# Reordering a neighbour-limited graph layer on one Trainium2 core: one landing rule for all loads, two count banks, the last tile in three loads

## The chip, the cores and the metric

The kernel runs on one core of a Trainium2 chip. A core has five engines that run side by side, each its own list of instructions in order: TensorE (PE, with PEld for its weight loads), VectorE (DVE), ScalarE (ACT), GpSimd (POOL) and SyncE (SP), which here only issues DMAs. Sixteen DMA engines move data between HBM and the on-chip memory SBUF; matrix products land in PSUM[...]. The metric is the device time in microseconds (us), lower is better; a time is the median of several runs.

## The reference

The layer normalises each of 4096 rows of 64 numbers, multiplies by a 64 x 64 matrix, and then sums over neighbours. Only the last 100 neighbours of a row count, and the one that lies k places before the last has the weight 2 to the power of minus k:

```python
    support = input @ weight
    mask = (adj != 0).astype(support.dtype)
    rank = jnp.cumsum(mask, axis=1)
    deg = rank[:, -1:]
    k = jnp.minimum(deg, float(MAX_NEIGH))
    pos = rank - (deg - k)
    w = mask * jnp.where(pos > 0, DECAY ** (k - pos), 0.0)
    out = w @ support + bias
...
    h = jnp.maximum(_layernorm(x, axis=-1), 0.0)
    x = x + _L0_gnn_ref(h, adj, L0_gnn_weight, L0_gnn_bias)
```

`adj` is a 4096 x 4096 matrix of float32, 67.1 MB, and nearly all that the kernel reads.

## The kernel before

**Tiles.** `adj` is taken in 32 tiles of 128 rows (2 MB each). A tile's 4096 columns are handled as eight blocks of 512. Two tiles make a pair u (16 pairs), four tiles a group g (8 groups) that shares one PSUM bank `acc`.

**Stages of a tile.** Each is a small function; the line of its instruction in the profile is given.

1. `load` (L295, SP): a DMA of the tile into one of four buffers `a_sb`. Tiles 0, 1, 28, 29, 30 and 31 are loaded in two halves, the others whole: 38 loads. A load into a buffer waits until the tile four earlier has been converted.
2. `convert` (L496, DVE): float32 to one byte per element, 64 or 65, into `m`.
3. `flip` (L506, DVE): transposes 32 x 32 blocks of packed words into the mask `mt`.
4. `totals` (L512, PE): counts the neighbours in each strip of the tile.
5. `split` (L517, ACT): takes the two bytes of each count apart, into `sums`.
6. `suffix` (L526, PE): sums the counts from each strip to the end of the row.
7. `clamp` (L530, DVE): limits them, into `behind`.
8. `place` (L538, L542, PE): adds to each element's strip count its place within the strip, into four PSUM banks `v`.
9. `weigh` (L551, ACT): four exponentials per tile turn `v` into weights `wk`; tile 31's are done in three parts (12 instructions), cut by `PARTED`.
10. `aggregate` (L559, PE): 32 products per pair, in eight tasks of four, add `wk` times the supports `hr` into `acc`.

**End of a group.** `drain` (L572, ACT) adds the bias, `turn_back` (L580, PE) transposes, `finish` (L586, DVE) adds the input, `store` (L590, SP) writes rows out. The last group is drained in two halves; there are nine drains, all on ACT, and four stores.

**Head.** Before the first weights the kernel builds constants (`constants`, and `order_of` on POOL, L375 to L389, which makes `near`, `rest` and `far` for `suffix`), normalises `x` (`turn`, `center`, `square`, `relu`, `spread`, `root`, `power`) and makes the supports (`support`, `scale`, `first`, `second`). The first weights' buffer also holds the normalisation's data, so that tile 2's weights wait for all four `second`.

**Order.** The order on each engine is made at build time by `plan()`: it holds a list of tasks with engine, duration (`hold`), time to result (`lag`), needs and buffers (`tasks()`), plays them in time, and at each step takes, among the tasks that could start within a small window (`WAIT`), the one with the lowest due time from the table `DUE`. For a load it reckons when its data is there from the data's size. PSUM is shared between `v` (`NV` = 6 banks), counts, suffixes and turned results `t` (`NB` = 1 bank) and `acc` (one bank). `warm` puts filler products on PE where the plan leaves it idle.

Of the kernel before, what the change touches and what calls it, by code (L numbers as in the profile page):

```python
# [8 lines left out]
F32 = mybir.dt.float32  # L9
F32R = mybir.dt.float32r  # L10
BF16 = mybir.dt.bfloat16
F16 = mybir.dt.float16
# [19 lines left out]
STEP = {t: 4 for t in (0, 1, 28, 29, 30, 31)}  # L32
LOADS = [(t, h, h + STEP.get(t, 8)) for t in TILES for h in range(0, 8, STEP.get(t, 8))]

PARTLY = {31}
PARTED = (0, 1, 0, 2), (1, 2, 0, 1), (1, 2, 1, 2)
DRAINS = [(g, 0, 4, True) for g in range(7)] + [(7, 0, 2, True), (7, 2, 4, True)]
STORES = [(0, 0, 16), (1, 0, 12), (1, 12, 14), (1, 14, 16)]
NA, NM, NT, NW, NV, NB = 4, 4, 4, 2, 6, 1

DUE = {
    "fetch": [-1003, -1847],
    "load": [65, 1148, 1192, 1344, 890, 882, 1059, 807, 177, 1469, 585, 426, -306, 496, -49, 266, 921, 615, 495, 273,
    509, 817, 887, 432, 1250, 832, 1156, 645, 31, 863, 872, 512, 638, 869, 1362, 792, 926, 1009],
    "load_rest": [-481],
    "turn": [-213, 892, -361, 828, -409, -147, 168, -107],
    "turned": [-404, -273, 1152, 128, 503, 511, 433, -263],
    "center": [-857, -641, -1350, -827],
    "square": [139, -1681, -2148, -2029],
    "relu": [217, 890, -64, 143],  # L50
    "spread": [-1274, -1134, -743, -201],
    "support": [458, 166, -823, -732],
    "scale": [31, 1087, -17, 582],
    "root": [-38],
    "power": [-305],
    "constants": [-1199, 288],
    "order_of": [1110],
    "count": [174],
    "counted": [-242],
    "first": [1030, 859, 446, 134],  # L60
    "second": [869, 310, 488, 149],
    "convert": [799, 235, 213, 621, 871, 221, 1137, 339, 665, 170, 840, 839, 269, 846, 1322, 763, 1208, 992, 1053, 1092,
    755, 1566, 506, 1283, 1017, 914, 1881, 1297, 1713, 1456, 1930, 1878, 1817, 1254, 2527, 1603, 1404, 1849],
    "flip": [755, -234, 295, -127, 442, -299, 314, 236, -95, 42, 943, 437, 1189, 848, 1722, 445, 670, 663, 1043, 1071,
    1018, 1159, 1502, 907, 1558, 1730, 1512, 1723, 625, 1907, 1701, 1739, 1719, 1519, 1418, 1515, 1365, 795],
    "totals": [163, 587, 208, 187, -888, 339, 133, -152, 475, 1157, 159, 135, 674, 545, 1071, 817, 439, 1024, 1281,
    1461, 443, 2052, 963, 1181, 926, 1932, 1537, 584, 1513, 1671, 1316, 1615],
    "split": [-294, -174, -1849, -575, -454, -698, -618, -971, -742, -275, 300, 6, -214, 155, -90, -143, 509, 616, 114,
    395, 584, 524, 615, 13, 506, 320, 818, 391, 1992, 1302, 1105, 460],
    "suffix": [265, 470, 626, 553, 76, 351, -120, 701, -560, 193, 222, 311, 159, 444, 810, -221, 772, 1294, 1743, 886,  # L70
    718, 429, 591, 1159, 1296, 2185, 1511, 1501, 2001, 1496, 2127, 1546],
    "clamp": [-739, 475, 354, 317, -585, 294, 102, -276, 538, 118, 920, -398, 130, 1157, 352, 866, 900, 81, -363, 492,
    698, 1569, 702, 757, 515, 1132, 736, 1149, 1495, 1590, 1729, 1541],
    "place": [841, 96, 498, 879, 824, 837, 808, 522, 1103, 1914, 1312, 1548, 862, 1225, 743, 1302, 1785, 1644, 1994,
    1697, 1566, 1560, 1577, 1633, 2537, 1922, 1847, 2364, 2393, 2364, 1714, 1845],
    "weigh": [1655, 1181, 868, 631, 1236, 404, 1584, 1443, 897, 269, 877, 841, 328, 1501, 418, 1096, 1670, 1095, 1290,
    1045, 1295, 1247, 1314, 999, 672, 1559, 1035, 1631, 1070, 1779, 1431, 1276, 2029, 1311, 1734, 1852, 1556, 1640,
    1599, 1881, 1168, 1820, 1423, 545, 1375, 1271, 1659, 2299, 2395, 2281, 2155, 2139, 2062, 2491, 1666, 1651, 1902,
    1875, 1618, 2485, 1751, 1754, 2523, 1796, 2184, 2358, 1409, 2593, 2132, 1541, 1713, 2047, 1583, 1456, 1562, 2282,
    1641, 1846, 1727, 2021, 2924, 2344, 2590, 1925, 1978, 2498, 1946, 1761, 2622, 1817, 2190, 1884, 1953, 2032, 2057,  # L80
    2381, 2020, 2701, 1854, 2394, 2313, 2255, 1976, 2259, 1957, 2012, 1591, 2429, 2382, 2260, 2365, 3172, 2928, 2044,
    3150, 1958, 2643, 2675, 2150, 3338, 2587, 2729, 2343, 2953, 1990, 2517, 2778, 3358, 2745, 2645, 3479, 2076, 3183,
    2758, 2299, 2866],
    "aggregate": [254, 1326, 1623, 59, 522, 1349, 93, 1245, 247, 484, 1268, 1686, 2132, 1190, 2358, 448, 974, 1308,
    1356, 611, 856, 1518, 486, 1545, 1236, 918, 398, 1827, 1513, 1406, 1117, 1500, 1296, 1193, 452, 1811, 1260, 1164,
    1961, 1568, 1038, 1010, 1127, 1422, 1532, 1050, 1941, 1756, 685, 1493, 1977, 1124, 1719, 1240, 1199, 787, 2328,
    1076, 2631, 1964, 1500, 1168, 989, 1906, 1959, 931, 1528, 1194, 1746, 1676, 1766, 1637, 1602, 1588, 2104, 1990,
    1832, 1942, 1495, 1697, 1592, 2020, 1907, 2085, 1379, 1230, 1622, 2213, 2061, 2515, 2853, 1453, 2287, 1736, 1377,
    1679, 1972, 1745, 1669, 2617, 3235, 2571, 1770, 2567, 1656, 2752, 2666, 1678, 2311, 2453, 2712, 2395, 2976, 2826,
    2628, 2119, 2143, 2488, 2511, 1602, 2160, 1962, 2594, 2032, 2291, 2585, 1920, 2821],  # L90
    "drain": [82, 374, 29, 620, 400, 1392, 1843, 1544, 1599],
    "turn_back": [572, 1129, 645, 1544, 2558, 1512, 1987, 1280, 2435],
    "finish": [79, 927, -547, 514, 1225, 592, 1061, 2342, 2532],
    "store": [8458, 8834, 7981, 9977],
}
WAIT = 250, 60, 150, 60, 0
PE, DVE, ACT, POOL, SP = range(5)


def tasks():  # L100
# [12 lines left out]
    for n, (t, _, _) in enumerate(LOADS):  # L113
        task("load", (n,), SP, n, 0, 0, [("convert", m) for m in range(n) if LOADS[m][0] == t - NA])
    task("load_rest", (), SP, 4, 0, 0, [("load", 2)])
    for h in range(2):
        for t0 in range(0, 16, 4):
            task("turn", (h, t0), PE, 0, 430, 680, [("fetch", h)], ("v", ("turned", h, t0)))
            task("turned", (h, t0), ACT, 0, 480, 640, [("turn", h, t0)])
    for n in range(4):  # L120
        task("center", (n,), PE, 1, 860, 1060, [("turned", 1, 12)], ("v", ("relu", n)))
        task("square", (n,), ACT, 1, 480, 640, [("center", n)])
        task("relu", (n,), ACT, 2, 480, 640, [("square", n)])
    for n in range(4):
        task("spread", (n,), PE, 2, 850, 1050, [("square", n)])
    for n in range(4):
        task("support", (n,), PE, 15, 890, 1090, [("relu", n), ("power",)], ("v", ("scale", n)))
        task("scale", (n,), DVE, 10, 610, 730, [("support", n), ("power",)])
# [7 lines left out]
    for i in (0, 2, 1, 3):  # L136
        task("first", (i,), ACT, 15, 520, 650, [("scale", i % 2 * 2 + 1), ("support", 3)])
        task("second", (i,), DVE, 15, 610, 740, [("first", i)])
# [496 lines left out]
```

## Time and profile before

| what | value |
|---|---|
| time, median of 3 runs | 188.82 us (188.42 to 188.97) |
| the profiled execution's own time | 188.37 us |
| its span in the profile | 186.7 us |
| PE busy | 164.9 us (88% of the span) |
| DVE busy | 146.8 us (79%) |
| ACT busy | 152.1 us (82%) |
| POOL busy | 18.9 us (10%) |
| HBM read | 68.19 MB |
| `weigh`, 124 full ones | 1081 ns each, 118.8 us in all |
| `convert`, 26 whole tiles / 12 halves | 2637 ns / 1375 ns each |
| `flip`, 26 whole tiles / 12 halves | 1241 ns / 706 ns each |

A profile is one execution; the 188.37 us contain its span of 186.7 us and what lies around it. Busy time is the time in which an engine has at least one instruction at work. Neighbouring instructions of one engine overlap a little in the records, so the distance from one start to the next (here called a slot) is shorter than a duration: four `weigh` in a row, 1081 ns each, start some 905 ns apart. The page cuts the span into 40 slices, one digit each, in tenths of busy share; the chain of work that ended last goes back from the last instruction to what released each one.

### The profile page before, as it was taken

What the parts mean: (1) busy time and instruction counts of PE and PEld (TensorE: products, weight loads), DVE (VectorE), ACT (ScalarE), POOL (GpSimd) and SP (SyncE); (2) the same over time, 40 slices, a digit from 0 to 9 for tenths busy, and PEclk for the clock granted to TensorE, in tenths of its full rate; (3) what the DMA queues carried; (4) which work ended last, traced back from release to release, by engine and by line L of the source; (5) the groups of instructions that cost most, each with busy time, mean ns of one, the idle gap of its engine ahead of it and who ended that gap; (6) DMA issues with size and microseconds to landing.
All of it is one profiled execution on the core that took longest, in us unless ns stands there. A gap on an engine that the chain in (4) does not pass through costs nothing.

```text
span 186.7 us, 4747 instructions
## 1 busy us (share of the span) xinstructions
PE 164.9 (88%) x2080; PEld 127.3 (68%) x2080; DVE 146.8 (79%) x152; ACT 152.1 (82%) x198; POOL 18.9 (10%) x57
## 2 busy tenths in 40 slices
PE   7999699647989899889998997999898979897982
PEld 5957367435857768667676775877775858685881
DVE  3187499999999997799797899879798989993100
ACT  2773176912999999699999999999969799999951
POOL 7899500000000000000000000000000000000000
PEclk9997569999999999999999999999999999999999
DMA  6999999999999999999999999999999999940020
GB/s 202 390 427 435 435 420 425 416 428 428 428 414 428 434 414 432 428 414 442 411 428 428 418 432 421 418 446 411 428 421 414 413 420 416 417 201 0 12 90 16
DMA packets 6597, 69.55 MB, mean 373 GB/s; under 512 B 944, under 2 KB 1200, under 8 KB 1712
## 3 DMA queue, kind: packets, MB, share of 16 engines
q1 hardware_dynamic: 6416, 69.21, 88.4%
q8 instruction: 16, 0.26, 0.6%
q10 hardware_dynamic: 160, 0.03, 0.1%
q14 instruction: 5, 0.04, 0.1%
HBM read 68.19 MB, written 1.05 MB: 371 GB/s over the span
## 4 chain that ended last, share of the span: by engine, by line
ACT 36%; PE 32%; DVE 15%; POOL 10%; issue 5%; POOLq 0%; ACTq 0%
ACT wk L551 29%; PE acc L559 19%; DVE m L496 7%; ACT sums L517 5%; PE ps L526 5%; PE po L580 3%; DVE mt L506 3%; PE v L542 2%; DVE behind L530 2%; PE v L538 2%; PE tot L512 2%; ACT acc_sb L572 1%; DVE wk L472 1%; DVE hr L482 1%; POOL where L414 1%
## 5 line engine op out<-in xcount | busy, mean ns | idle before, releaser
L551 ACT ACTIVATE wk<-v 128x1024 fp32r<-128x1024 uint8 (+2 forms) x136 | 123.2, 1028 | 2.3 <-PE v L542 2.1
L496 DVE TENSOR_SCALAR m<-a_sb 128x4096 uint8<-128x4096 f32 (+1 forms) x38 | 84.8, 2238 | 5.0 <-DMA a_sb<-in_adj_dram 5.0
L559 PE MATMUL acc<-wk,hr 128*128 128x256 f32 x512 | 74.6, 291 | 3.7 <-ACT wk L551 2.2
L559 PEld LDWEIGHTS acc<-wk,hr 128*128 128x128 f32 x512 | 64.0, 188 | 10.6 <-ACT wk L551 4.3
L506 DVE STREAM_TRANSPOSE mt<-m 128x1024 f32<-128x1024 f32 (+1 forms) x38 | 40.7, 1072 | 0.4
L517 ACT ACTIVATE sums<-tot 128x512 f16<-128x512 uint8 x32 | 20.3, 634 | 16.4 <-PE tot L512 16.4
L530 DVE TENSOR_SCALAR behind<-ps,excess 128x256 f16<-128x256 f32 x32 | 15.4, 481 | 14.1 <-PE ps L526 13.9
L526 PEld LDWEIGHTS <-far 128*128 128x128 f16 x224 | 17.9, 101 | 1.9 <-POOL far L389 1.0
L526 PE MATMUL ps<-sums,far 128*128 128x224 f16 (+6 forms) x224 | 18.5, 225 | 0.7 <-POOL far L389 0.7
L512 PE MATMUL tot<-mt,band 128*32 128x256 f16 x256 | 13.5, 288 | 5.3 <-DVE mt L506 4.3
L538 PE MATMUL v<-behind,where 32*128 32x256 f16 x256 | 13.6, 276 | 2.7 <-DVE behind L530 2.3
L542 PE MATMUL v<-mt,tri 32*32 32x512 f16 x512 | 14.5, 401 | 0.0
L586 DVE TENSOR_TENSOR xr<-po,xr 128x256 f32<-128x256 f32 (+1 forms) x9 | 3.5, 393 | 12.4 <-PE po L580 12.3
L423 PE MATMUL none<-junk 128*128 128x256 bf16 x74 | 11.9, 318 | 1.1 <-DVE junk L307 1.1
L512 PEld LDWEIGHTS <-band 128*32 128x32 f16 x256 | 4.1, 95 | 11.3 <-DVE mt L506 6.1
L423 PEld LDWEIGHTS <-junk 128*128 128x128 bf16 x87 | 8.8, 109 | 3.8 <-DVE junk L307 1.1
L526 PE MATMUL ps<-sums,near 128*128 128x256 f16 x32 | 9.2, 286 | 2.0 <-ACT sums L517 1.8
L572 ACT ACTIVATE acc_sb<-acc,bias_sb 128x512 f32<-128x512 f32 (+1 forms) x9 | 6.1, 679 | 5.4 <-PE acc L559 5.4
L580 PE MATMUL po<-both,acc_sb 128*128 128x64 f32 x64 | 8.7, 275 | 1.9 <-DVE behind L530 1.3
L580 PEld LDWEIGHTS po<-both,acc_sb 128*128 128x128 f32 x64 | 7.8, 191 | 2.8 <-DVE behind L530 1.5
L538 PEld LDWEIGHTS <-where 32*128 32x128 f16 x256 | 4.5, 92 | 7.5 <-issue 4.7
L542 PEld LDWEIGHTS <-tri 32*32 32x32 f16 x512 | 4.4, 88 | 6.9 <-issue 6.9
(86 smaller groups left out, 91.0 us busy)
## 6 DMA issues: line engine op xcount, KB each, us to landing
a_sb<-in_adj_dram SPq DMA_DIRECT2D x26, 2048.0 KB, 15.3
a_sb<-in_adj_dram SPq DMA_DIRECT2D x12, 1024.0 KB, 13.2
xr<-in_x_dram SPq DMA_DIRECT2D x2, 512.0 KB, 3.9
out_dram<-xr SPq DMA_DIRECT2D x1, 512.0 KB, 17.1
out_dram<-xr SPq DMA_DIRECT2D x1, 384.0 KB, 2.3
out_dram<-xr SPq DMA_DIRECT2D x2, 64.0 KB, 1.6
w<-in_L_gnn_weight_dram ACTq DMA_DIRECT2D x2, 16.0 KB, 5.8
bias_sb<-in_L_gnn_bias_dram SPq DMA_DIRECT2D x1, 0.2 KB, 18.8
```

Source lines behind the costliest of these rows:

```text
L423: nc.tensor.matmul(idle[0][:, idle[1]:idle[1] + 2 * P], junk[:, :P], junk, start=not accs, stop=not accs, skip_group_check=True)
L496: nc.vector.tensor_scalar(words[n][:, :(k1 - k0) * P, :].rearrange("p (h q) e -> p h e q", q=P), tiles[t][:, k0 * W:k1 * W].rearrange("p ( ...
L506: nc.vector.transpose(to[:, k0:k1], m_v.rearrange("p (h c l) -> p h c l", c=4, l=SUB))
L512: nc.tensor.matmul(tot[SUB * c:SUB * (c + 1), :V], band[:, SUB - 12 - 4 * a:2 * SUB - 12 - 4 * a], masks[t][:, c, :, a], start=(a == 0), s ...
L517: nc.scalar.activation(sums8[t], pts.pop((t, "n"))[:, :V].bitcast(U8).rearrange("p (i f) -> p f i", f=4)[:, :2, :], AF.Copy, bias=-136.0)
L526: nc.tensor.matmul(o, l, m, start=(k == 0), stop=(k == len(todo) - 1), skip_group_check=True)
L530: nc.vector.tensor_scalar(behind[t], pts.pop((t, "s"))[:, :V], excess, float(MAX_NEIGH), op0=ALU.subtract, op1=ALU.min)
L538: nc.tensor.matmul(vs[t, j][:, a, :], where[q, a, :], behind[t][q, :], start=(a == 0), stop=False, skip_group_check=True)
L542: nc.tensor.matmul(vs[t, j][SUB * c:SUB * (c + 1), :, :], tri[q, q], masks[t][q, c, :, :].rearrange("p i a -> p a i"), start=False, stop=T ...
L551: nc.scalar.activation(wts[u][:, s0:s1, 8 * a0:8 * a1, i, j, :], v[:, s0:s1, 8 * a0:8 * a1], AF.Exp, scale=-LN2, bias=-38.0 * LN2)
L559: nc.tensor.matmul(accs[g][:, at:at + 2 * P], hr[:, h * 4 + 2 * a + s, :, :].rearrange("p s d -> p (s d)"), wts[u][:, s, 8 * a + h].rearra ...
L580: nc.tensor.matmul(pts["o", d][:, k, :], sums[d][:, k * P:(k + 1) * P], both, start=True, stop=True)
```

## The change

The order of all engines is made anew, with another table `DUE` and with other durations and needs in `tasks()`. Its parts:

- A load's data counts as there some time after the nominal end of its transfer, by a rule `late` that is the same for every tile and grows over the run (850, 1750, 3200 ns).
- Tiles 28, 29 and 30 are loaded whole; tile 31 is loaded in three pieces (blocks 0 to 3, 4 and 5, 6 and 7), each flipped by itself. There are 36 loads.
- Each whole tile is converted in two instructions of four blocks, and flipped in one.
- `t` has two banks (`NB` = 2), of which a tile uses half (`half()`), and `v` has five (`NV` = 5). `behind` has four buffers.
- `weigh`'s parts of tile 31 go by blocks (0 to 3, 4 and 5, 6 and 7), and `aggregate`'s eight tasks of a pair go by block.
- `order_of` runs on DVE; `constants` for `where` works on 8 columns in place of 256 and spreads them in its last instruction; the bias is loaded by two DMAs; `both` and `less` are made in a task `stack`.
- The drains stay as they were: all nine on ACT. `encode` and `take` are new functions for doing weights on DVE, and `HALF_UNITS` for half tiles; both sets are empty, so that neither is used.

The diff's core:

```diff
-STEP = {t: 4 for t in (0, 1, 28, 29, 30, 31)}
-LOADS = [(t, h, h + STEP.get(t, 8)) for t in TILES for h in range(0, 8, STEP.get(t, 8))]
-
-PARTLY = {31}
-PARTED = (0, 1, 0, 2), (1, 2, 0, 1), (1, 2, 1, 2)
+CUTS = {0: ((0, 4), (4, 8)), 1: ((0, 4), (4, 8)), 31: ((0, 4), (4, 6), (6, 8))}
+HALF_UNITS = set()
+
+LOADS = [(t, h0, h1) for t in TILES for h0, h1 in CUTS.get(t, ((0, 8),))]
+PIECES = LOADS
+UNITS = [(t, 0, 8) for t in TILES]
+
+PARTS = {31: ((0, 4), (4, 6), (6, 8))}
+QUICK = set()
...
-NA, NM, NT, NW, NV, NB = 4, 4, 4, 2, 6, 1
+NA, NM, NT, NW, NV, NB = 4, 4, 4, 2, 5, 2
...
-    task("order_of", (), POOL, 1, 3500, 3600, [("constants", 0)])
+    task("order_of", (), DVE, 1, 2950, 3050, [("constants", 0)])
+    task("stack", (), DVE, 2, 600, 700, [("order_of",)])
...
+def late(at):
+
+    return 850 if at < 17000 else 1750 if at < 104000 else 3200
...
             lag = max(landed - at, 2450) + dma_ns(f, args)
             landed = at + lag
+            lag += late(landed)
...
-    bhpool = ctx.enter_context(tc.tile_pool(name="bhpool", bufs=2))
+    bhpool = ctx.enter_context(tc.tile_pool(name="bhpool", bufs=4))
...
-        nc.sync.dma_start(bias_sb[:D], bias.rearrange("(d o) -> d o", o=1))
+        b = bias.rearrange("(d o) -> d o", o=1)
+        for d0, d1 in ((0, 8), (8, D)):
+            nc.sync.dma_start(bias_sb[d0:d1], b[d0:d1])
...
     def order_of():
-        vec = nc.gpsimd
+        vec = nc.vector
...
+    def half():
+        return ps_t.tile([P, V], F32, tag="t", name="sums")
...
-    def convert(n):
-        t, k0, k1 = LOADS[n]
-        words[n] = bpool.tile([P, N // E, E], U8, name="m8")
+    def convert(n, i):
+        t, h0, h1 = PIECES[n]
+        if i == 0:
+            words[n] = bpool.tile([P, N // E, E], U8, name="m8")
+        k0, k1 = 4 * i, min(4 * i + 4, h1 - h0)
...
-    def aggregate(u, k):
+    def aggregate(u, h):
...
-        a, s = k // 4, k // 2 % 2
-        for h in range(k % 2 * 4, k % 2 * 4 + 4):
-            nc.tensor.matmul(accs[g][:, at:at + 2 * P], hr[:, h * 4 + 2 * a + s, :, :].rearrange("p s d -> p (s d)"),
-                             wts[u][:, s, 8 * a + h].rearrange("p i j r -> p (i j r)"), start=(k == h == 0),
-                             stop=(k == h == 7), skip_group_check=True)
+        order = order_in(u)
+        for e in range(4):
+            a, s = e // 2, e % 2
+            nc.tensor.matmul(accs[g][:, at:at + 2 * P], hr[:, h * 4 + e, :, :].rearrange("p s d -> p (s d)"),
+                             wts[u][:, s, 2 * h + a].rearrange("p i j r -> p (i j r)"), start=(h == order[0] and e == 0),
+                             stop=(h == order[-1] and e == 3), skip_group_check=True)
```

With the new order the instructions near the end stand as follows (a number is the tile, for `aggregate` the pair and the block):

```
VectorE  convert 30 (two), clamp 29, flip 30, convert 31 (three), clamp 30, flip 31 (three), clamp 31, finish (three)
ScalarE  weigh 29 (first), split 30, weigh 29 (two), drain 6, weigh 29 (last), weigh 30 (first), split 31, weigh 30 (three), weigh 31 (four of the first part), drain 7, weigh 31 (eight), drain 8
TensorE  aggregate 13.3 to 13.5, place 29, aggregate 13.6, totals 30, aggregate 13.7, suffix 30, place 30, totals 31, aggregate 14.0 to 14.2, suffix 31, turn_back 6, aggregate 14.3, place 31, aggregate 14.4 to 14.7, 15.0, 15.1, turn_back 7, aggregate 15.2 to 15.7, turn_back 8
```

Before, tile 30 is converted and flipped in two halves with tile 29's clamp behind the second convert, the drain of group 6 stands one `weigh` earlier, and TensorE turns group 6 back after it has placed tile 31.

## The prediction

> **What bounds the kernel now.** I read four views in this order: the row of DMA slices, the times at which single loads land, the waits of ScalarE, and last the chain that ended last.
>
> The DMA row of the page and stretches of 1 us near its end (columns: length, then busy time of PE, PEld, DVE, ACT and POOL with counts, the granted clock, the DMA share, GB/s):
>
> ```profile
> DMA  6999999999999999999999999999999999940020
> ...
> 162.00:163.00 1.00, 1.00 (x10) 1.00 (x10) 0.96 (x2) 1.00 (x3) 0.00 (x0) 1.00 0.96 397
> 164.00:165.00 1.00, 1.00 (x12) 0.93 (x8) 1.00 (x3) 1.00 (x3) 0.00 (x0) 1.00 0.74 303
> 166.00:167.00 1.00, 1.00 (x15) 0.90 (x8) 0.97 (x2) 1.00 (x2) 0.00 (x0) 1.00 0.36 147
> ```
>
> The DMA engines are full from about 4 us to 163 us and then thin out, one after another, over some 3 us. No reordering of compute can end this stream earlier; only what comes after it can shrink.
>
> The line of the loads, asked for the two halves of tile 30 and then of tile 31: issue times, and issue to landing.
>
> ```profile
> L295 SPq DMA_DIRECT2D a_sb<-in_adj_dram x2: 327/376/426, 145.6 to 146.0; - x2
> DMA to landing us min/median/max: 13.3/14.3/15.4
> ...
> L295 SPq DMA_DIRECT2D a_sb<-in_adj_dram x2: 328/377/426, 149.7 to 150.1; - x2
> DMA to landing us min/median/max: 14.1/15.2/16.3
> ```
>
> Tile 30 is complete at 146.0 + 15.4 = 161.4 us and tile 31 at 150.1 + 16.3 = 166.4 us; 186.7 - 166.4 = 20.3 us of the span come after the last mark.
>
> ScalarE in order of time, three of its lines:
>
> ```profile
> 45.46 0.60 ACT L517 ACTIVATE sums<-tot 128x512 f16<-128x512 uint8 x1 [3.44 <-PE tot L512]
> 46.09 7.44 ACT L551 ACTIVATE wk<-v 128x1024 fp32r<-128x1024 uint8 x8
> ...
> 138.96 1.03 ACT L551 ACTIVATE wk<-v 128x1024 fp32r<-128x1024 uint8 x1 [1.52 <-PE v L542]
> ```
>
> Tile 2's weights begin at 46.1 us, when the last of the four "second" operations is done. From then ScalarE works off a backlog nearly without a pause, until at 138.96 us it waits 1.5 us for PE: there it has caught up with the data. So the slow start is already paid back 48 us before the end.
>
> The chain that ended last, from 170.8 us (start, length, what):
>
> ```profile
> 168.92 1.84 ACT wk L551 x2
> 170.80 1.69 PE acc L559 x12
> 172.49 0.62 PE ps L526 x9
> 173.11 1.04 PE acc L559 x8
> 174.15 0.33 PE v L538 x8
> 174.47 0.38 PE v L542 x14
> 174.85 1.04 PE po L580 x8
> 175.89 1.49 PE acc L559 x12
> 177.46 0.48 ACT acc_sb L572
> 177.99 0.74 PE acc L559 x4
> 178.72 0.39 PE po L580 x4
> 179.11 3.38 PE acc L559 x28
> 182.58 0.48 ACT acc_sb L572
> ```
>
> From tile 29's last weights the end is one piece of PE work: 64 products of pairs 14 and 15, tile 31's suffix and placing, two turns back and one drain between them, 182.48 - 170.80 = 11.7 us without a gap worth naming, and then a fixed 4.2 us (drain, turn back, finish, store). What the change does to the end is what it does to this start, 170.80 us.
>
> [...] the share falls over 3 us, 0.96 to 0.36, before tile 31 may be read. [...] the trace shows what one bank costs, waits of PE of 0.6 to 0.8 us for a clamp (1.3 us for the turns back, 1.0 us for totals). [...] this is the rival below on five placing buffers, and the trace of before, with six, has 4.4 us of ScalarE idling over 30 tiles.
>
> **The change, part by part.** *Head.* The 13 operations of order_of took POOL from 13.6 to 21.6 us and held up the first suffix (21.68 us); on VectorE, at about 0.2 us each, they are 2.9 us, inside the 3.93 us that it waits there for the first load. POOL's 128x256 operations (1.2, 2.0, 0.7, 2.1 us) shrink to eight columns. By the new order tile 2's weights can begin near 38 us: VectorE reaches the third tile's converts at 23.3, then per the listed order two more tiles and the four "second" operations, each with its old duration. That is 8 us earlier, and worth nothing at the end, since before had caught up at 138.96. Without that cover (if it had not caught up) it would be worth up to the whole 8 us.
>
> *Converts.* 26 whole-tile converts of 2.64 us become pairs of 1.33 us (the pair at 152.48 takes 2.66): +0.5 us over the run, hidden in VectorE's spare time: per tile 2.55 (pair) + 0.40 (clamp) + 1.15 (flip) + 0.1 (finish) = 4.2 us of slots against 4.9 us between marks. Tiles 28 to 30 go back to one load and one flip (1.15 for 2 x 0.64). *Loads.* A tile in halves came every 5.0 us (161.4 to 166.4); whole ones are spaced some 4.9 (67.1 MB over the full stretch), so tile 30's mark comes about 0.2 us earlier, estimate, 161.2; the last mark is then 166.3 with one more small transfer. VectorE read the last half only at 167.35, a microsecond after its mark, so the third piece by itself gains nothing. *The split bias load, drains.* One more tiny transfer among 40 on SP; it lands far ahead of the first drain. All drains are on ScalarE in both: nothing. *Weights.* Same shapes (1024, and 512, 256, 256 elements for tile 31), same 512 products.
>
> *The order at the end*, step by step, with slots from the trace (start to next start). Tile 30 marked 161.2; its two converts 2.55: 163.75; clamp of 29 there (164.29 before); placing starts 0.54 after a clamp does: 164.3; weights start 0.79 after a placing does: 165.1 (165.9 before). ScalarE: weights 0.905, split 0.47, two weights 1.81, drain of group 6 0.57, so tile 29's last weights start at 165.1 + 3.75 = 168.85; its products may start 1.1 us after that (169.70 to 170.80 before): 169.95. VectorE meanwhile: clamp 0.40 and flip 1.15 of tile 30 to 165.3, three converts of tile 31 2.55 to 167.85, clamp of 30 to 168.25, three flips 1.3 to 169.55; totals of 31, which stand before the products on PE, 0.1 + 0.34: 170.0. Both roads meet at 170.0, against 170.80: **0.8 us earlier**. Behind it PE has the same 11.7 us in slightly changed order (turn back of group 6 before tile 31's placing), split of 31 ready at 171.1 for a suffix due at 171.5, placing due at 173.6 with its clamp at 172.4. Sum: span 186.7 - 0.8 = 185.9; the profiled execution would be 188.37 - 0.8 = 187.6; that run lies 0.45 below the median, 188.82 - 0.8 = **188.0 us**.
>
> *New wait.* With five placing buffers instead of six, tile t's placing waits for the third of tile t-1's four weights, not the second; on PE, products and totals queue behind it, and ScalarE waits for those. In my chain the third weights of 29 end at 168.3, just when tile 30's clamp (167.85 + 0.54) allows its placing, and ScalarE wants the result at 169.75: cover 169.75 - 0.79 - 168.4 = 0.55 us. Bounds: 0, or one weights slot, 0.9 us, per tile. I take 0. The second count bank gives back at most the 3.8 us of such waits summed over the run (1.0 + 1.3 + 1.5), none of them in the last chain: 0.
>
> **The rivals.** *A, forecast, 188.0*: the start of the last PE piece moves 0.8 us. *B, nothing: 188.8.* The two roads to 170.0 have no slack between them; small pieces cost a fixed part that the trace of before does not show (it has no 1024-column convert or flip). Four such operations at 0.2 us more each cancel the 0.8. For it: 2 x 0.71 against 1.24 for flips shows a fixed part of 0.18. Against it: slots, not durations, count on a busy engine, and there two halves take 1.28 for 1.15. *C, slower: 190.6.* Five placing buffers. PE must place (0.8 us) while ScalarE has only one weights (0.9) and perhaps a split left; if PE stands in a group of products (up to 1.5 us) at that moment, ScalarE idles s each tile. It has 4.9 - 4.3 = 0.6 us per tile to give and starts 38 us with some 5.6 us to recover over 28 tiles (0.2 each): above s = 0.4 it never catches up and each further 0.1 costs 2.8 us. At s = 0.5 that is 2.8 - 0.8 = 2 us, 190.6 to 190.8. Against it: before idled only 0.15 per tile. *D, better: 187.0*: the 3 us over which the DMA engines finish shrink by 1[...]; tile 30's mark and all behind it come 1 us earlier still. The mirror of it, 1 us later, is 189.0 and lies in the range.
>
> **How the numbers follow.** A 0.50, B 0.23, C 0.19, D 0.08. 0.3% is 0.57 us, what this kernel's measurement can tell: 188.25 and 189.4 are the borders. A falls below 188.25 with two chances in three (0.33) and else within; D is faster (0.08); B is within but for a few chances each way; C is slower, with 0.04 of B. Faster 0.43, same 0.34, slower 0.23. Range: 187.0 (D) to 190.0, which leaves the worse half of C outside. For A and D alone it is 187.0 to 188.5.
>
> **What would show it.** Right: last mark within 0.3 us of 166.3; ScalarE's weights of tile 2 near 38 us; VectorE waiting for loads in the middle of the run; the last unbroken PE stretch starting near 170.0 and ending near 181.7. B: it starts after 170.5 with flips ending after 170. C: PE "v <- ACT wk" waits of tenths of a microsecond in every tile. Wrong altogether: a last mark moved by over 0.5 us, or the 11.7 us changed.

## The result

| | before | after |
|---|---|---|
| time, median (20 runs each) | 188.75 us (188.17 to 189.10) | 190.17 us (188.39 to 191.93) |
| profiled execution, its span | 188.37, 186.7 us | 190.7, 188.7 us |
| first product of pair 14 | 170.80 us | 171.25 us (predicted 170.0) |
| the PE piece from there to its last product | 11.7 us | 13.2 us (predicted 11.7) |

After against before: 1.0076 [1.0059, 1.0093], slower; 188.0 was predicted. (A time is the median of all executions, a ratio rests as a rule on the mean of those within 1.5% of a kernel's fastest, so the two need not agree.) The 2.0 us between the two spans are 0.45 at the start of the piece and 1.5 inside it. Against the span that was forecast, 185.9 us, the 2.8 us are 1.25 at the start and 1.5 inside. The profiled execution of after is one of its slower ones.

The loads did what was predicted. VectorE after (start, length, what, idle time before it and its releaser):

```profile
161.15 2.72 DVE L542 TENSOR_SCALAR m<-a_sb 128x2048 uint8<-128x2048 f32 x2 [0.35 <-DMA a_sb<-in_adj_dram]
163.99 0.48 DVE L587 TENSOR_SCALAR behind<-sums,excess 128x256 f16<-128x256 f32 x1
```

Tile 30 is read on its mark at 161.15 us (predicted 161.2), and tile 29 is clamped at 163.99 (163.75). The last load lands near 166.0 us (166.3). So the DMA side is right to 0.3 us, and what fails comes after it. TensorE after, from there on, and then the chain that ended last:

```profile
161.10 0.74 PE L635 MATMUL acc<-wk,hr 128*128 128x256 f32 x4 [0.17 <-ACT wk L615]
161.78 0.41 PE L560 MATMUL sums<-mt,band 128*32 128x256 f16 x8
162.12 1.21 PE L635 MATMUL acc<-wk,hr 128*128 128x256 f32 x8
...
163.80 1.66 PE L635 MATMUL acc<-wk,hr 128*128 128x256 f32 x12
165.39 0.40 PE L597 MATMUL v<-behind,where 32*128 32x256 f16 x8
```

```profile
169.71 0.57 ACT acc_sb L648
170.28 0.92 ACT wk L615
171.21 0.04 issue
171.25 2.46 PE acc L635 x12
173.71 1.20 PE sums L581 x9
174.91 1.16 PE sums L656 x8
```

In the first, 24 products of pair 13 start at 161.10, when ScalarE has made tile 27's last weights. Tile 29's placing stands behind them and starts at 165.39, 1.4 us after its clamp began. In before 8 products stood between tile 29's clamp and its placing, which started 0.77 us after it:

```profile
163.94 1.18 PE L559 MATMUL acc<-wk,hr 128*128 128x256 f32 x8
164.29 0.48 DVE L530 TENSOR_SCALAR behind<-ps,excess 128x256 f16<-128x256 f32 x1
165.06 0.40 PE L538 MATMUL v<-behind,where 32*128 32x256 f16 x8
```

In the second view of after, 12 products take 2.46 us (1.69 before) and a suffix 1.20 (0.62 before). The granted clock shows a reason, which a later run bears out (after the comma the busy times of PE, PEld, DVE, ACT and POOL with counts, then the clock, the DMA share and GB/s):

```profile
170.00:171.00 1.00, 0.92 (x29) 0.26 (x24) 0.50 (x2) 1.00 (x2) 0.00 (x0) 1.00 0.00 0
171.00:172.00 1.00, 0.75 (x5) 0.75 (x6) 0.00 (x0) 1.00 (x3) 0.00 (x0) 0.92 0.00 0
172.00:173.00 1.00, 1.00 (x7) 1.00 (x6) 0.00 (x0) 1.00 (x3) 0.00 (x0) 0.50 0.00 0
...
175.00:176.00 1.00, 1.00 (x9) 1.00 (x10) 0.43 (x1) 0.36 (x1) 0.00 (x0) 0.87 0.00 0
```

For 3.4 us, 171.85 to 175.26, the granted clock of TensorE is 0.50; in the 3.4 us before it is 1.00. The clock's records show two more such stretches of 3.4 us, at 28.5 and 55.8 us. In the profile of before the clock is 0.50 for 10.2 us on end, 16.2 to 26.4, in the head, and 1.00 from there to 186 us.

The rivals C and B of the prediction are judged by these waits of after (who waits, for whom, us in total, times, longest):

```profile
ACT wk L615 <- PE v L601: 14.9, 13, 3.8
...
DVE m L542 <- DMA a_sb<-in_adj_dram: 7.5, 11, 2.3
...
PE v L597 <- ACT wk L615: 1.8, 6, 0.6
```

VectorE waits for loads in the middle of the run, as forecast, and ScalarE idles more (2.1 us in 2 before). TensorE's placing waits for a buffer only 1.8 us in 6 waits, not in every tile. But three of the six lie at 151, 160 and 170 us, and the first of these, for tile 26, is a step of the chain that ended last:

```profile
151.07 0.37 PE L597 MATMUL v<-behind,where 32*128 32x256 f16 x5 [0.50 <-ACT wk L615]
```

Tile 27's count and placing queue behind it, so the five buffers can have cost up to 0.5 us of the late start; that they did is not shown. B's sign is there as well, a start after 170.5 with flips that end at 170.5. Small pieces account for little of it: tile 30's two converts took 2.72 us, where 2.55 was reckoned. Then tile 30's clamp waited for a suffix on TensorE:

```profile
168.74 0.48 DVE L587 TENSOR_SCALAR behind<-sums,excess 128x256 f16<-128x256 f32 x1 [0.53 <-PE sums L581]
```

### The profile page after: what moved, and what is told of

The parts are those of the page before. It is cut to its first block, busy times and chain, and to the rows that moved or that the text cites. A ratio compares the mean times of both kernels' runs of the same rounds, so it can differ in the third digit from the quotient of the medians.

```text
span 188.7 us, 4792 instructions
## 1 busy us (share of the span) xinstructions
PE 168.1 (89%) x2090; PEld 129.8 (69%) x2090; DVE 150.2 (80%) x190; ACT 153.9 (82%) x198; POOL 6.8 (4%) x43
## 4 chain that ended last, share of the span: by engine, by line
PE 42%; ACT 23%; DMA 17%; DVE 13%; issue 2%; SPq 1%; DVEq 0%; ACTq 0%
PE acc L635 23%; ACT wk L615 18%; DMA a_sb<-in_adj_dram 17%; DVE m L542 8%; PE sums L581 6%; PE v L601 4%; PE sums L656 4%; PE v L597 3%; ACT sums L568 3%; PE sums L560 2%; DVE mt L552 2%; DVE behind L587 1%; ACT acc_sb L648 1%; DVE wk L513 1%; SPq L334 1%
## 5 line engine op out<-in xcount | busy, mean ns | idle before, releaser
L542 DVE TENSOR_SCALAR m<-a_sb 128x2048 uint8<-128x2048 f32 (+1 forms) x65 | 85.7, 1375 | 7.8 <-DMA a_sb<-in_adj_dram 7.5
L635 PEld LDWEIGHTS acc<-wk,hr 128*128 128x128 f32 x512 | 64.8, 190 | 11.7 <-issue 7.3
L552 DVE STREAM_TRANSPOSE mt<-m 128x1024 f32<-128x1024 f32 (+2 forms) x36 | 40.0, 1118 | 0.3
L568 ACT ACTIVATE sums<-sums 128x512 f16<-128x512 uint8 x32 | 20.1, 630 | 6.6 <-PE sums L560 6.3
L587 DVE TENSOR_SCALAR behind<-sums,excess 128x256 f16<-128x256 f32 x32 | 15.1, 477 | 11.3 <-PE sums L581 11.2
L581 PE MATMUL sums<-sums,far 128*128 128x224 f16 (+6 forms) x224 | 18.5, 225 | 0.0
L560 PE MATMUL sums<-mt,band 128*32 128x256 f16 x256 | 13.1, 284 | 1.4 <-DVE mt L552 1.3
L581 PE MATMUL sums<-sums,near 128*128 128x256 f16 x32 | 9.2, 286 | 1.7 <-ACT sums L568 1.2
L656 PE MATMUL sums<-both,acc_sb 128*128 128x64 f32 x56 | 8.4, 296 | 2.2 <-ACT sums L568 2.2
L656 PEld LDWEIGHTS sums<-both,acc_sb 128*128 128x128 f32 x56 | 7.4, 206 | 3.1 <-ACT sums L568 2.4
L581 PE MATMUL sums<-sums,rest 128*128 128x256 f16 x32 | 9.0, 281 | 0.0
```

The costliest lines, as they stand in the source:

```text
L542: nc.vector.tensor_scalar(words[n][:, k0 * P:k1 * P, :].rearrange("p (h q) e -> p h e q", q=P), tiles[t][:, (h0 + k0) * W:(h0 + k1) * W].r ...
L552: nc.vector.transpose(to[:, h0:h1], m_v.rearrange("p (h c l) -> p h c l", c=4, l=SUB))
L560: nc.tensor.matmul(tot[SUB * c:SUB * (c + 1), r], band[:, SUB - 12 - 4 * a:2 * SUB - 12 - 4 * a], masks[t][:, c, r, a], start=(a == 0), st ...
L568: nc.scalar.activation(sums8[t][:, :, r], pts.pop((n, "n")).bitcast(U8).rearrange("p (i f) -> p f i", f=4)[:, :2, r], AF.Copy, bias=-136.0)
L581: nc.tensor.matmul(o, l, m, start=(k == 0), stop=(k == len(todo) - 1), skip_group_check=True)
L587: nc.vector.tensor_scalar(behind[n][:, r], pts.pop((n, "s"))[:, r], excess, float(MAX_NEIGH), op0=ALU.subtract, op1=ALU.min)
```

## The experiments

Times are medians, ratios against before in the same session.

### Clock or order at the end

The letters of the theories in this part are not those of the prediction's rivals. T1 held that the half clock in the tail is the loss, T2 the place of the placings in TensorE's order, T3 the missing sixth placing buffer. First, zero products as filler before tile 30's placing and before pair 14:

```diff
+        for i in range(6 if n == 30 else 0):
+            nc.tensor.matmul(vs[n, 0][:, :4], junk[:, :P], ...)
...
+            for i in range(3 if g == 7 else 0):
+                nc.tensor.matmul(accs[g][:, at:at + 2 * P], junk[:, :P], junk, start=True, stop=True, ...)
```

> The changed kernel with nine filler products of zeros on PE in its last lull: six ahead of tile 30's placing, three ahead of pair 14's first product. Theory T1 (the PE clock halves for some 3.4 us in the tail, because PE does too little from 166.8 to 171.3 us, and that costs 1.5 of the 2.0 us by which the changed kernel's profiled execution is longer): the clock stays whole after 170 us, the last PE piece takes 11.7 to 11.9 us again in place of 13.2, and the time falls from 190.2 to 188.6 us with far less spread between runs. Theory T2 (the late start of the last PE piece, by order and buffers, is the loss): no change, 190.2 +- 0.3, or slower by the fillers' 1.0 us.

Second, the order: two blocks of products moved behind the odd tile's placing.

```diff
+    for u in range(9, 14):
+        late_ones = [s for s in steps if s[2] == "aggregate" and s[3] in ((u, 4), (u, 5))]
...
+        k = next(i for i, s in enumerate(steps) if s[2] == "place" and s[3] == (2 * u + 3,)) + 1
+        steps[k:k] = late_ones
```

> The changed kernel with PE's order changed for pairs 9 to 13: the products of blocks 4 and 5 stand behind the placing of the odd tile two pairs' tiles on, not ahead of it. T2: every odd tile's placing comes some 1.0 us earlier, ScalarE's waits for placing shrink, pair 14's first product starts near 170.2 in place of 171.25, and the time falls by about 1.0 us to 189.2. T1: the start may move, but the PE clock still halves in the tail; the time stays at 190 +- 0.5 with the same spread.

Both together:

> Both edits in one kernel. If the two losses are separate and add up: 190.2 - 1.5 - 1.0 = 187.7 us, under the kernel before (188.8). If the earlier start only turns into another wait: as with the fillers alone, 188.6.

Before with the pool of `v` cut from six to five banks, the order untouched:

```diff
-    ps_v = ctx.enter_context(tc.tile_pool(name="ps_v", bufs=NV, space=bass.MemoryType.PSUM))
+    ps_v = ctx.enter_context(tc.tile_pool(name="ps_v", bufs=5, space=bass.MemoryType.PSUM))
```

> The kernel before, its order unchanged, with five placing buffers allotted where six were planned. Theory T3 (the sixth buffer is what the changed kernel misses): ScalarE's waits for placing rise from 2 us towards the 15 us of the changed kernel, and the time rises by 1 us or more to 190. T1 and T2: under 0.4 us slower, 188.8 to 189.2, since before works off a backlog on ScalarE and placing is seldom what it waits for.

| run | time | ratio |
|---|---|---|
| tail fillers | 191.06 us | 1.0111 [1.0078, 1.0144] |
| placing first | 191.87 us | 1.0134 [1.0085, 1.0184] |
| both | 192.51 us | 1.0210 [1.0168, 1.0253] |
| before, five buffers | 198.63 us | 1.0540 [1.0496, 1.0583] |

All expectations of a gain failed. With the fillers the clock is 1.00 in every microsecond from 160 to 186 us and the piece is short again, but it starts at 172.70 us: an earlier half-clock stretch lasted about twice as long, 6.8 us by an estimate from the mean clock (0.973 of 188.5 us makes 10.2 us of half clock, 3.4 of it in the head; the page shows 0.5 and 0.8 in the two slices from 56.5 to 66.0 us, 0.7 and 0.9 in after), and the whole loop came 1.45 to 2 us later from tile 8 to the end. So T1 is right on the length of the piece, and its gain was lost elsewhere. Placing first brought tile 29's placing to 0.54 us after its clamp, but made the loop itself slower: 40.2 us from the last weights of tile 20 to those of tile 28, against 38.7 in after. The waits for a placing buffer rose with it from 1.8 to 4.1 us:

```profile
PE v L597 <- ACT wk L615: 4.1, 10, 0.7
```

So this run does not tell the order from the buffers. Five buffers cost before 9.9 us:

```profile
PE v L538 <- ACT wk L551: 6.3, 13, 1.1
```

(0.4 us in before). Some of the 9.9 us may be clock: in its profiled execution the mean granted clock is 0.89 from 70 to 90 us, 0.94 from 90 to 110 and 0.97 from 150 to 165, where that of before has 1.00. This points to T3, but for the order of before only.

### The buffers, with new plans

Here theory B held that the reuse of five placing buffers holds the loop up, C that half clock alone makes the difference, and O, later, that the order itself does. Before planned anew with five and two, that part of the change alone:

```diff
-NA, NM, NT, NW, NV, NB = 4, 4, 4, 2, 6, 1
+NA, NM, NT, NW, NV, NB = 4, 4, 4, 2, 5, 2
```

> The kernel before, planned anew with five placing buffers and two count banks (that part of the change alone). Theory B: slower than the kernel before, 190 us or more, but less than the 198.6 of five buffers under the unchanged order; waits of the placing for the weights of some us in total where before has 0.4. Theory C: within 1 us of the kernel before as long as the clock stays whole after 30 us.

After planned anew with six and one (`totals` also needs the suffix two tiles back):

> The kernel after, planned anew with six placing buffers and one count bank (the split of PSUM undone, all else kept). Theory B (five placing buffers set the loop's own pace: where no load was waited for, the run with tail fillers took 4.50 us a tile from tile 12 to 20 and 4.83 from 20 to 28, the kernel before 4.30 and 4.67): about 4.3 and at most 4.7 us a tile where no load is waited for, the first product of the last pair starts at 170.0 to 170.6 us, time 188.0 to 189.0 us. Theory C (the clock's half-speed stretches alone make the difference): the time is set by whether a lull trips the clock before the last pair, not by the buffers: 189.5 us or more if the lull before the last pair stays, whatever the buffers.

Three further runs try six placing buffers with two counts, which lie in the halves of one bank:

```diff
+    bank, halves = ps_t.tile([P, 2, V], F32, name="bank"), []
...
     def half():
-        return ps_t.tile([P, V], F32, tag="t", name="sums")
+        halves.append(0)
+        return bank[:, len(halves) % 2, :]
```

After in its own order; after planned anew for six and two; before planned anew for six and two:

> The kernel after with every instruction in its order, but six placing buffers: the two count tiles lie in the two halves of one bank. Theory B (the reuse of five placing buffers holds the loop up): the placing's waits for the weights (1.8 us in 6 in the kernel after) go, the loop's pace from tile 20 to 28 falls from 4.83 us towards the 4.67 of the kernel before where no load is waited for, the first product of the last pair starts at 170.0 to 170.6 us, time 188.0 to 189.2 us. Theory O (the order written for five buffers is what is slow: an odd tile's placing stands behind 24 products that need the weights of the odd tile before): with six buffers and the same order the pace stays at 4.8 us a tile and the time at 190.2 us within 0.6.

> As the run with six buffers and the same order, but planned anew for six placing and two count tiles (the due times are those of the change). The plan still puts the placing of tiles 27 and 29 behind 24 products, so Theory O: about 190 us, 189.5 to 191. Theory B: 188.0 to 189.2 us.

> The kernel before, planned anew for six placing tiles and two count tiles that share a bank: the second count tile alone, without giving up a placing buffer. Theories B and O both: no gain at the end, as the last marks set it, 188.0 to 189.3 us; more than 190 us would mean that the due times of the kernel before fit its own buffers only, and that any new plan costs.

| run | time | ratio |
|---|---|---|
| before, five and two | 198.10 us | 1.0499 [1.0463, 1.0535] |
| after, six and one | 215.88 us | 1.1414 [1.1350, 1.1478] |
| after, own order, six and halves | 200.94 us | 1.0512 [1.0478, 1.0547] |
| after, planned for six and halves | 192.31 us | 1.0158 [1.0123, 1.0193] |
| before, planned for six and halves | 194.72 us | 1.0322 [1.0304, 1.0341] |

Before with five buffers stays at 198 us whether planned anew or not, just inside what B expected. But the last row shows that planning before anew costs something by itself: with six placing buffers it takes 194.72 us, where 188.0 to 189.3 was expected. The rest say nothing clean on the buffers. With six and one, after's due times meet a single count bank, which they were not made for; whether that is the reason for 215.88 us was not tried. With the halves, VectorE waits for other users of the bank, which after does not show (own order, six and halves; columns as above):

```profile
DVE behind L590 <- PE bank L659: 7.2, 2, 5.6
DVE behind L590 <- ACT sums L571: 4.4, 3, 2.4
```

So whether after would be faster with a sixth buffer could not be tried without another cost.

### Early fillers

The early lulls filled as well, with the tail fillers and without:

```diff
     def place(n):
+        warm(16 if n == 0 else 0)
...
+        po = half()
+        for i in range(18 if d == 0 else 0):
+            nc.tensor.matmul(po, junk[:, :P], junk, start=True, stop=True, ...)
```

> The tail fillers of the first run again, and 16 zero products more ahead of the first placing and 18 ahead of the first turn back, where the kernel after has lulls of 2 to 3 us followed by half clock. Theory C: no half clock after 25 us, the loop is not 1.5 us late any more, the first product of the last pair starts by 171.3 us, the last PE piece is 11.7 us, time 188.3 to 189.0 us. Theory B: the clock is whole, yet the loop has no slack and the time stays at 189.5 us or more.

> The early fillers alone (16 ahead of the first placing, 18 ahead of the first turn back), nothing in the tail. Theory C: the early half-clock stretches go and the loop is up to 1.5 us earlier between tiles 8 and 16, but it then waits for loads, so the start of the last pair's products stays at about 171.2 us with half clock behind it in most executions: 190.0 us, the same as the kernel after within 0.4 us. Theory B: 190 us too. If early delays persist instead, as they did in the run with tail fillers, 188.5 to 189.2 us.

191.26 us (1.0135 [1.0097, 1.0174]) and 191.99 (1.0174 [1.0141, 1.0207]): slower. TensorE with early and tail fillers:

```profile
55.71 3.44 PE L661 MATMUL sums<-junk 128*128 128x256 bf16 x18 [2.18 <-ACT sums L568]
58.94 1.39 PE L664 MATMUL sums<-both,acc_sb 128*128 128x64 f32 x8
60.27 0.40 PE L600 MATMUL v<-behind,where 32*128 32x256 f16 x8
```

The fillers waited for the same release as the turn back (2.18 us), so the lull stayed, the clock fell (to a mean of 0.6 in the slice from 56.7 to 61.4 us of the page), and the 18 took 3.44 us, where 16 like them take 1.91 at whole clock (after, 22.53 us). They stood in front of tile 6's placing, which came 3.5 us later than in after (56.76). Misplaced, they became a dose of delay, and that is of use. End of a tile's last weights, in us from the start of the span:

| | tile 8 | tile 12 | tile 20 | tile 28 | 20 to 28, per pair |
|---|---|---|---|---|---|
| before | 74.91 | 94.18 | 128.56 | 165.89 | 9.33 |
| after | 71.06 | 90.43 | 126.96 | 165.65 | 9.67 |
| tail fillers | 73.05 | 92.46 | 128.50 | 167.09 | 9.65 |
| early and tail fillers | 73.48 | 92.87 | 128.86 | 167.48 | 9.66 |
| early fillers | 74.83 | 94.27 | 130.32 | 168.92 | 9.65 |
| before, five buffers | 76.99 | 100.67 | 137.84 | 178.07 | 10.06 |

A pair's loads take 9.81 us (the first converts of tiles 28 and 30 in after, 151.34 and 161.15). From tile 20 to 28 after's loop runs at 9.65 to 9.67 us a pair. In after itself VectorE waits for loads in this stretch, so that its number alone says little; in the three runs with fillers it waits for none after 109 us, and the pace is the same. There it is the loop's own, and it wins back only 0.15 us a pair. It was not so all along: from tile 12 to 20 the same three runs took 9.0 us a pair, and before 8.6. With early fillers it stands at tile 12 where before does (94.27 and 94.18); sixteen tiles on, before is 3.0 us ahead. Theory L: the loop of after has a chain of its own (an odd tile's last weights, 24 products, the suffix and placing of the next odd tile, then ScalarE), nearly as long as the loads.

### The head

`order_of` moved to VectorE in before, nothing else; and moved back to GpSimd in after, nothing else:

```diff
     def order_of():
-        vec = nc.gpsimd
+        vec = nc.vector
```

> The kernel before with its order-of-sums constants on VectorE in place of GpSimd, nothing else moved. The prediction's step: tile 2's weights start 3 to 8 us sooner, converts then wait for loads, and the end gains nothing or as little as the last marks allow: first product of the last pair at 170.0 to 170.8 us, 188.0 to 188.8 us. If the delays of the head persist to the end in the kernel before as they do in the kernel after: 187.5 us or less.

> The kernel after with its order-of-sums constants on GpSimd again, all else in its order. Theory L: the head is 2 to 4 us later, the loop does not make it up, and the end is later by nearly as much: 191.0 to 193.5 us. The prediction's step (a later head is made up before the end): 190.2 us within 0.5.

Before with the new head takes 187.85 us, 0.9976 [0.9955, 0.9997]: faster than after, and than before by a margin just clear of the noise. Tile 2's weights start at 44.40 us, only 1.7 us sooner than in before. Its waits for loads and its chain:

```profile
DVE m L496 <- DMA a_sb<-in_adj_dram: 14.1, 18, 4.3
```

```profile
167.22 1.37 DVE m L496
168.58 0.37 DVE behind L530
168.96 0.04 issue
169.00 0.40 PE v L538 x8
169.40 0.37 PE v L542 x14
169.77 0.34 PE tot L512 x8
170.11 1.61 PE acc L559 x12
```

The chain now comes from the last load, which is converted, clamped and placed; pair 14 starts at 170.04 us (170.11 in the chain) and its last product ends at 181.73, 11.7 us later. This is the prediction's end, to the tenth, without its order: a chance match. In before VectorE waited for loads 4 times, all at tiles 0 and 1; here 18 times. So before had not caught up with the data, and ScalarE's pause at 138.96 us was one for TensorE, with no wait for a load behind it.

After with the head on GpSimd takes 190.35 us (1.0069 [1.0050, 1.0087]), as after, and not the 191.0 to 193.5 us of theory L. But its head isn't later: tile 2's weights start at 37.45 us (37.38 in after). So it doesn't test what a late head costs; it shows that the move alone is worth nothing in after. Its profiled execution, however, met no half clock in the tail:

```profile
PEclk9999999999996999999999999999999999999999
```

```profile
170.05 0.92 ACT wk L615
170.97 0.04 issue
171.02 1.68 PE acc L635 x12
172.70 0.62 PE sums L581 x9
```

The same order on PE, the same start (171.02), and a piece of 11.5 us: span 186.8 us where after has 188.7, time 188.57. This execution's mean granted clock is 0.991, and that of after's profiled one, with three stretches of 3.41 us, 0.973: a stretch takes 0.9% off the mean (half of 3.41 us in 187), so all executions can be sorted by it. By this estimate it tells how many stretches an execution had, not where they lay:

| mean clock | 0.979 and more | 0.970 to 0.977 | 0.969 and less |
|---|---|---|---|
| after | 188.39 (1) | 189.71 to 190.70 (11) | 190.08 to 191.93 (8) |
| after, head on GpSimd | 188.57 to 189.45 (7) | 190.27 to 191.05 (12) | 191.82 to 191.92 (3) |
| before (27 of a later session) | none | 188.22 to 189.24 (16) | 188.33 to 188.77 (11) |

In after's order every further step of 0.9% in the clock costs 1.1 to 1.6 us between medians (one of these steps rests on after's single execution of 188.39 us); in before, whose profiled half clock lies in the head (16.2 to 26.4 us), none.

### A shorter loop

Half of the products of pairs 8 to 12 left out, without and with the tail fillers; pairs 13 to 15 are whole.

```diff
-        for e in range(4):
+        for e in range(2 if 8 <= u <= 12 else 4):
```

> The kernel after with half of the products of pairs 8 to 12 left out (64 of 128 blocks' halves stay per pair as two of four products in each block), pair 13 to 15 whole. Theory L (the loop's own chain, weights of an odd tile, 24 products, suffix, placing of the next odd tile, weights, takes 9.6 us a pair against 9.8 us of loads, and so recovers nothing): with about 1.5 us of products less in the chain it has slack, VectorE waits for loads at every tile from 18 on, place 29 starts at 164.3 to 164.9 us and the last pair's products at 170.0 to 170.5 us, 0.8 to 1.2 us sooner than in the kernel after; time 188.3 to 189.5 us, by whether the lull before them halves the clock. Rival (the tail alone is late, by the order of tiles 29 to 31): start at 171.2 as in the kernel after, 190.2 us.

> The same with the tail fillers of the first run added. Theory L with the clock: start of the last pair's products at 170.0 to 170.8 us, clock whole after it, 187.6 to 188.4 us: both failed terms of the prediction undone give its number back. Rival: 190 us or more.

188.93 us (1.0014 [0.9992, 1.0035]) and 188.44 us (0.9997 [0.9982, 1.0013]). The chain without fillers:

```profile
158.39 0.37 DVE behind L587
158.76 0.04 issue
158.81 0.40 PE v L597 x8
...
168.66 0.92 ACT wk L615
169.58 0.04 issue
169.62 1.68 PE acc L635 x12
```

VectorE waits for loads 15 times (11.0 us), tile 29's placing starts at 163.8 instead of 165.4, again 0.54 us after its clamp, and pair 14 at 169.62, 1.6 us sooner than in after. Some 0.5 us of that is the loads': tile 30 is converted from 160.66 us here, from 161.15 in after and from 161.50 in the run with fillers, whose pair 14 starts at 170.56. From that convert to pair 14 the two runs take 8.96 and 9.06 us, after 10.10. So a shorter loop is worth some 1.1 us at the start of the piece, as theory L has it. The waits for a placing buffer fell too, to 0.6 us in 1, so that these runs show the loop's chain to be too long, and not whether by its products or by the buffers. The run with fillers just missed its range of time (188.4). Sorted by mean clock, its executions of 0.970 to 0.977 have a median of 188.40 us (7) and those of 0.969 and less of 188.51 (15): with slack in the loop and fillers in the tail, a further step of the clock costs next to nothing, 0.1 us. The rival, that only the last three tiles are ordered badly, would have left 171.2.

### The clock in the faster version

Fillers in front of two lulls of before with the new head:

```diff
     def totals(t):
+        warm({3: 8, 4: 14}.get(t, 0))
```

> The kernel before with its order-of-sums constants on VectorE (187.85 us) and 8 and 14 zero products more ahead of the totals of tiles 3 and 4, in lulls of 1.4 and 2.1 us after which its clock fell to half at 40.8 us. Theory (a half-clock stretch in the loop costs up to 1.5 us where loads leave no slack): no half clock between 25 and 180 us, span 185.9 us or less, time 187.0 to 187.7 us, few executions above 188.5. Rival (the stretch at 41 us is made up before the end): 187.85 us as without the fillers.

188.05 us, 0.9973 [0.9952, 0.9994]: the rival holds, no gain over 187.85. The stretch at 41 us went (the slice from 41.8 to 46.5 us of the page had a clock of 0.7, here every slice from 23.4 to 149.8 us has 0.9 or more), and another came in the profiled execution at 152.7 us (0.85 in the microsecond from 152). With the fillers, and without them (before with the new head):

```profile
151.00:152.00 1.00, 1.00 (x29) 0.59 (x28) 0.96 (x3) 1.00 (x2) 0.00 (x0) 1.00 1.05 426
...
153.00:154.00 1.00, 1.00 (x7) 1.00 (x6) 1.00 (x2) 1.00 (x3) 0.00 (x0) 0.50 1.02 426
```

```profile
151.00:152.00 1.00, 1.00 (x29) 0.57 (x27) 0.95 (x3) 1.00 (x2) 0.00 (x0) 1.00 1.01 410
...
153.00:154.00 1.00, 1.00 (x11) 0.96 (x10) 1.00 (x2) 1.00 (x3) 0.00 (x0) 1.00 0.99 410
```

Up to there both lie within 0.1 us of each other, and their last loads land within 0.1 us too; but tile 27's placing comes 1.6 us later and pair 14's start 1.45 us later (171.49 against 170.04). So the price of a late half-clock stretch is no peculiarity of after. Of its 22 executions 13 have a mean clock of 0.979 or more and take 187.14 to 188.14 us; the other 9 take 188.47 to 189.77.

## Why the prediction was wrong

- **Loads, marks, head.** Tile 30's mark, the last mark and tile 2's weights (37.38 us for "near 38") came as predicted, and VectorE waits for loads in the middle.
- **"A slow start is already paid back", head worth nothing: wrong.** The pause at 138.96 us was read as catching up with the data. VectorE had never waited for a load there; ScalarE waited for TensorE. The head alone gives before 0.75 us by the medians, 0.24% by the ratio. What after gains by its earlier head was not measured.
- **"Placing starts 0.54 after a clamp does: 164.3": the first failed step.** In before this is the distance for tile 28, for which TensorE stood waiting; tile 29's own was 0.77 us. In the listed order tile 29's placing stands behind 12 products that follow the suffix, and behind 12 more that wait for tile 27's last weights (161.06), and this was put at nothing. The distance is 1.40 us for tile 29, and 1.3 us or more for every odd tile from 21 on. Measured 165.39, 1.1 us late, and pair 14 starts at 171.25, 1.25 us late. Half the products in pairs 8 to 12 brought the distance back to 0.54 us and won some 1.1 us.
- **"The same 11.7 us": the second failed step.** It measured 13.2 us, as a stretch of half clock (0.50 from 171.85 to 175.26 us) fell into it. Without one it is 11.5 to 11.7 us (before, before with the new head, after with the head on GpSimd, half products), so the amount of work was right and its speed was not. In after 19 of 20 executions have the mean clock of the profiled one, 0.973, or less; in how many a stretch fell into the piece is not recorded. The one with the clock at 0.979 took 188.39 us.
- **The new wait taken as 0.** It is 1.8 us in 6 waits, with 0.50 us of it in the last chain, where the prediction had none. Five buffers cost before 9.5 to 9.9 us, clock and new plan included; what they cost after through the order made for them stays open. A placing moved forward made the loop slower (10.0 us a pair) and these waits longer.
- **The second count bank.** The 3.8 us that it could give back count one wait twice, as weight load (1.5) and as product (1.3): 2.3 us. It did not matter, as the prediction put the gain at the end at 0.
- **Rivals.** C's 190.6 (188.8 and its 2 us would be 190.8) is near the 190.17, but what the runs show is another mechanism: no stall of 0.4 us in each tile, but a loop with 0.15 us of slack a pair from tile 20 on, and the clock on top. So its nearness is in part luck.

## What to carry to other kernels

A loop that only just kept up with its loads (9.65 us a pair against 9.81) passed most of a delay on to the end: with tail fillers 2.0 us at tile 12 were still 1.4 at tile 28. Ask for the loop's own pace in a stretch where it waits for nothing (here 9.65 against 9.33 us a pair) and not only for its idle time. In a new order, follow a step through what stands before it on its engine; a distance measured in the old order does not carry over. And the piece of TensorE work behind a lull ran at half clock in one profile and at whole in another of the same order of products (the first 12 took 2.46 and 1.68 us): price it both ways, and sort the executions by their mean clock before explaining a spread, keeping in mind that the mean does not say where a stretch lay.

## What the runs showed of the hardware

In the traces of before and after the granted clock has two values, 1.00 and 0.50. In after it is 0.50 three times, for 3.413 us each, from 28.49, 55.79 and 171.85 us; these lie 8 and 34 times 3.413 us apart, so the three stand on one grid. In before it is 0.50 once, for 10.24 us from 16.15, three times 3.413. Counted from the start of the span, 28.49 us in after is eight steps of 3.413 us and 1.2 us more, 16.15 us in before four steps and 2.5 us; whether that difference is why one kernel's executions fall into groups was not tested.

What brings the half clock on is not settled. In after TensorE was busy for 0.70, 0.52 and 0.92 of the three microseconds from 168 us, and the clock fell to 0.50 at 171.85; in before with the new head and fillers it fell at 152.7 us after 0.79, 0.42, 0.63 and 1.00 from 148 us, and without the fillers, nearly the same 0.78, 0.38, 0.65 and 1.00 left it at 1.00. So the busy time of these microseconds alone does not tell the two apart, and what does was not shown. In the 3.41 us before the fall in after (168.44 to 171.85) TensorE was busy for 2.31 us and no gap was longer than 0.6 us, so this fall came without a long pause. The six fillers that ran in the tail's lull (0.81 us from 170.00, run with tail fillers) went with a clock of 1.00; the 18 that waited for the same release as the work behind them took 3.44 us and came too late.
